# Moving a block's routing counts one step later in a mixture-of-experts kernel

## The chip, the cores and the metric

The kernel runs on one core of a Trainium2 chip. The metric is device time in microseconds, from the start of the program to its end. Before the change three runs took 1308.88, 1309.06 and 1309.46 us; the median is 1309.06 us. A core has a matrix engine (TensorE, "PE" in the profile, with its weight loads as "PEld"), three engines for elementwise work (VectorE "DVE", ScalarE "ACT", GpSimd "POOL"), and SyncE ("SP"), which in this kernel issues nearly all plain DMA transfers. Each engine works through its own instructions in a fixed order.

## What is computed

For 8192 tokens of width 512, the layer normalizes the input `x`, adds a random-feature attention of the normalized tokens, and adds a mixture of 64 experts, of which every token uses 8 (with 256 places per expert), plus a shared expert. Cut to what matters here:

```python
xn = _layernorm(x)
# attention: features of every token times features of a weight
feats = 1/sqrt(512) * AB * exp(xn @ (ab*proj).T - 0.5*|xn|^2 * ab^2)
attn  = feats @ weights.T
# routing
scores      = sigmoid(xn @ router_w)              # 64 experts in 8 groups
masked      = scores of the 4 best groups, 0 elsewhere
topk_w, topk_idx = top_k(masked, 8);  topk_w = 2.5 * topk_w / sum(topk_w)
onehot = one_hot(topk_idx.reshape(-1), 64)
prior  = cumsum(onehot, axis=0) - onehot          # how many came before, per expert
pos    = prior at the chosen expert               # the token's place in the expert's list
# each expert works on its list; results are weighted and added back
out = x + attn + experts(xn) + shared_expert(xn)
```

The running count of tokens per expert (`prior`) is what the changed step builds, block by block.

## The kernel before

The 8192 tokens are cut into 16 blocks of 512 (`NB`, `TB`), a block into four pieces of 128. All matrix products are done in three parts (upper times upper, upper times rest, rest times upper), which `products` (L103) issues; `upper` (L97) makes the upper part on ScalarE and `rest` (L100) the remainder on VectorE.

**Two phases.** In the first, to about 400 us, `dense` (L517) does the shared expert and the attention for the even blocks 0, 2, ..., 14, and beside it every block, odd ones too, is normalized, turned and routed. In the second, the 64 experts run one after another (`hidden` L796, `down` L817), with the attention of the odd blocks and the last block's dense part put between them.

**Steps.** `dense` is a generator. For one even block it yields ten times: n = 0 and 1 after the two halves of the shared expert's hidden layer (24 products each, `ps_gu`), n = 2 to 5 after four feature chunks (12 products each, `ps_f`), n = 6 to 9 after four output pieces (18 products each, `ps_o`). After every yield the main loop (L867) calls `routing(step)` (L853), with steps counted 0 to 79; so two blocks are routed for each even block of dense work, one every five steps (`GAP`).

**What `routing` does in a step.** It first advances every running `look_up` generator by one yield, in order of blocks. Then, on the block's first step (second for block 1), it starts `look_up` for the next block. In its third step of five it computes the statistics and normalizes one block ahead (`normalize`, L299, into the `xw` tiles), and in the second it loads a block two ahead (`load_tokens`).

**Stages of `look_up(b)` (L345), one per step:**

- turn: 16 transposes into `ps_x`, split into `xT_h` (ScalarE) and `xT_l` (VectorE, L101); odd blocks store both to `turned`
- logits: 8 products into `ps_l`, copied to `lt`; the squared norms are stored by four small DMAs (`as_row`, L258)
- back: four transposes into `ps_lt`, sums `lg`, exponentials into the `xw` tiles
- groups: the penalty that rules out all but the 4 best groups
- top 8: `top`, `mask_r`, and the running sums `prior_r` (L437) and `taken` (L440), all on VectorE
- a step in which nothing is done
- **counts**: five products into `ps_bu` (L447, L458), of which the first gives counts before the block and the others the counts within it; the second kind is copied to `cu` (ScalarE, L466) and stored to `upto` (L467); then the shares of the chosen experts (L469 to L475), and the two stores of the normalized rows and their shares to `xnw` (L478)
- `begun` (L486): two VectorE updates from the first count

Counted from a block's turn as step 0, the counts come at step 6. For odd blocks from 3 on the turn follows the dense step n = 0, so that the counts come at n = 6; for even blocks the turn follows n = 5 and the counts come at n = 1 of the next dense block.

**What sets the order.** The program order gives each instruction a rank. The framework that builds the program then plays it through with estimated durations and gives each engine the ready instruction of the best rank; the result is a fixed order per engine. An instruction whose data are ready early can thus go before others that stand before it in the program. `behind(a, b)` (L119) forces a to come after b: `counted` comes after the last product of the dense step (L454), and so do the transposes of `ps_lt`.

**Buffers that matter.** `ps_sm` has two PSUM buffers, shared by `ps_x` (every second one), `ps_l`, `ps_lt`, `ps_bu` and, later, `ps_fu` and `ps_y`. `mask` and `prior` have one buffer each, `top` two. The `xw` tiles have four buffers of which each block takes two, from its normalization to the landing of its `xnw` stores.

**The hand-over.** In the last dense block, after n = 8, `chunks` (L691) turns `begun` into row numbers, and `find` and `gather` (L699, L752) start to look up each expert's tokens with indirect DMAs. They need the last block's counts.

Of the kernel before, what the change touches and what calls it, by code (L numbers as in the profile page):

```python
# [32 lines left out]
NB = T // TB  # L33
# [20 lines left out]
def rfs_attention_moe_kernel(  # L54
# [290 lines left out]
    def look_up(b):  # L345
# [94 lines left out]
        nc.vector.tensor_tensor(taken, prior[:, NS - 1, :], mask[:, NS - 1, :], ALU.add)  # L440
        yield
        yield


        both = ps_sm.tile([P, 2, TB // 2], FP, tag="sm", name="ps_bu")
# [210 lines left out]
    for rc in range(RC):  # L656
        pool, tag = ((ps_sm, "sm"), (ps_tr, "tr"))[rc // 2]
        ps_w.append(pool.tile([P, H], FP, tag=tag, name="ps_f"))
        projected(parts(wT, KC), rc, ps_w[rc])
    late = look_up(0)  # L660
    next(late)
    upper0 = last["upper"]
# [190 lines left out]
    def routing(t):  # L853

        for b in sorted(fronts):
            if next(fronts[b], fronts) is fronts:
                del fronts[b]
        b, k = divmod(t + GAP, GAP)
        if k == (b == 1) and b < NB:
            fronts[b] = look_up(b)  # L860
            next(fronts[b])
        if k == GAP - 3 and b + 1 < NB:
            normed[b + 1] = normalize(b + 1, *roots(b + 1, statistics(xbs[b + 1])))
        if k == 1 and b + 2 < NB:
            xbs[b + 2] = load_tokens(b + 2)
# [140 lines left out]
```

## Time and profile before

| What | Value |
|---|---|
| Median of three runs | 1309.06 us |
| Profiled execution | 1309.75 us |
| its span | 1308.0 us |
| DVE busy in the span | 71% |
| DMA, mean over the span | 259 GB/s |
| First and last count product (L447), start | 48.9 and 392.8 us |

The profile is of one execution. Its views used here are: the page (busy time by engine, granted TensorE clock in 40 slices), the timeline (start, duration, engine, line, operation, what is written and read, and in brackets the idle time just before and what ended it), the waits (who waited for whom), the chain of waits (followed back from the last instruction), and the times at which DMA transfers landed. In the timeline equal neighbours are merged ("x4" is four instructions). The end of a matrix product is modelled, so its start is the sounder number: 512-column products that follow each other without a gap start 0.227 us apart.

### The profile page before, as it was taken

To read this page: it belongs to the slowest core of one execution; us is meant where nothing else is said; L and a number is where in the kernel's file an instruction comes from. 1 tells how busy PE (TensorE), PEld (TensorE's weight loads), DVE (VectorE), ACT (ScalarE), POOL (GpSimd) and SP (SyncE) were. 2 spreads that over 40 slices of the span, in tenths; PEclk is the share of its full clock that TensorE was granted. 3 is DMA by queue.
4 is the path that set the end of the run, shared out by engine and by line. 5 is a ranking of instruction groups with operands and counts; after the bars stand their busy time and mean duration, and the time that the engine had idled before them with its cause. 6 is when DMAs were issued, how large, how long until landed. Compare 5 with 4: busy or idle time off the path is not lost.

```text
span 1308.0 us, 21401 instructions
## 1 busy us (share of the span) xinstructions
PE 1295.1 (99%) x7648; PEld 1136.1 (87%) x7648; DVE 925.9 (71%) x1922; ACT 644.1 (49%) x1017; POOL 587.0 (45%) x692
## 2 busy tenths in 40 slices
PE   8999999999999999999999999999999999999998
PEld 6888888888888988999999999999999999988886
DVE  7978768867765776678677677777776776643555
ACT  5643544454432555566566465656665565540111
POOL 3122022123106766777677767767766654210000
PEclk9999999999999999999999999999999999999999
DMA  7655675675586989999999999999999999784995
GB/s 255 242 209 207 242 282 200 240 286 212 198 306 191 308 236 322 263 288 274 303 288 251 282 290 270 264 302 290 275 257 297 286 260 238 204 240 167 319 319 193
DMA packets 189498, 338.61 MB, mean 259 GB/s; under 512 B 15952, under 2 KB 87632, under 8 KB 189392
## 3 DMA queue, kind: packets, MB, share of 16 engines
q1 hardware_dynamic: 153456, 245.93, 54.4%
q0 software_dynamic: 35936, 91.32, 29.8%
q8 instruction: 60, 0.98, 0.3%
q14 instruction: 46, 0.38, 0.1%
HBM read 220.66 MB, written 104.99 MB: 249 GB/s over the span
## 4 chain that ended last, share of the span: by engine, by line
PE 87%; DVE 7%; DMA 3%; SPq 1%; issue 1%; ACT 1%; POOL 0%; ACTq 0%; DVEq 0%
PE ps_gu L108 41%; PE ps_e L108 13%; PE ps_o L108 12%; PE ps_fu L108 6%; PE ps_y L108 5%; PE ps_t L773 3%; PE ps_f L108 3%; PE ps_x L333 2%; PE ps_l L366 1%; DMA xb<-in_L_attn_x_dram 1%; DVE st L277 1%; DVE f L495 1%; SPq L264 1%; DVE xT_l L101 1%; DVE fT L101 1%
## 5 line engine op out<-in xcount | busy, mean ns | idle before, releaser
L831 POOL DMA_INDIRECT out_dram<-ye,who x128 | 232.7, 1818 | 181.5 <-ACT ye L830 120.8
L108 PE MATMUL ps_gu<-gT,gu_h 128*128 128x256 f32 x2048 | 292.5, 285 | 0.0
L108 PEld LDWEIGHTS ps_gu<-gT,gu_h 128*128 128x128 f32 x2048 | 265.4, 190 | 8.9 <-ACT gu_h L98 4.7
L703 POOL DMA_INDIRECT at<-upto,line x128 | 131.9, 1030 | 76.0 <-DVE first_of L697 37.3
L101 DVE TENSOR_TENSOR gu_l<-gu,gu_h 128x1024 fp32r<-128x1024 f32 x128 | 155.0, 1221 | 14.3 <-ACT gu_h L98 13.4
L108 PE MATMUL ps_gu<-gT,gu_l 128*128 128x256 f32 x1024 | 164.9, 283 | 0.0
L756 POOL DMA_INDIRECT xg<-xnw,who x128 | 141.7, 1107 | 40.0 <-issue 30.0
L108 PE MATMUL ps_e<-d_h,ehT 128*128 128x512 f32 x512 | 147.8, 390 | 0.0
L108 PEld LDWEIGHTS ps_gu<-gT,gu_l 128*128 128x128 f32 x1024 | 142.6, 191 | 3.4 <-DVE gu_l L101 0.7
L98 ACT CAST gu_h<-gu 128x1024 fp32r<-128x1024 f32 x128 | 132.1, 1047 | 0.0
L830 ACT ACTIVATE ye<-ps_e,we 128x512 f32<-128x512 f32 x128 | 87.6, 687 | 84.5 <-PE ps_e L108 84.2
L108 PEld LDWEIGHTS ps_e<-d_h,ehT 128*128 128x128 f32 x512 | 94.7, 188 | 18.8 <-ACT d_h L98 0.2
L98 ACT CAST ehT<-sg 128x512 fp32r<-128x512 f32 x64 | 39.9, 623 | 123.1 <-DVE sg L503 112.0
L248 POOL TENSOR_TENSOR a<-rstd,ve 128x4 f32<-128x4 f32 x45 | 10.2, 227 | 200.5 <-DVE rstd L244 198.0
L503 DVE SCALAR_TENSOR_TENSOR sg<-sg,ps_gu 128x512 f32<-128x512 f32 x64 | 43.9, 686 | 72.1 <-PE ps_gu L108 72.0
L101 DVE TENSOR_TENSOR gT<-ps_t,gT 128x512 fp32r<-128x512 f32 x128 | 82.0, 682 | 17.1 <-ACT gT L98 17.1
L101 DVE TENSOR_TENSOR d_l<-d,d_h 128x1024 fp32r<-128x1024 f32 x64 | 78.2, 1221 | 11.7 <-ACT d_h L98 11.6
L509 ACT ACTIVATE f<-f,ab 128x512 f32<-128x512 f32 x64 | 46.3, 723 | 73.1 <-DVE f L495 72.4
L108 PE MATMUL ps_o<-fW_h,fT 128*128 128x512 f32 x288 | 79.8, 391 | 0.2 <-ACT fT L98 0.2
L108 PE MATMUL ps_e<-d_l,ehT 128*128 128x512 f32 x256 | 79.2, 390 | 0.0
L108 PE MATMUL ps_o<-d_h,hT 128*128 128x512 f32 x256 | 79.1, 396 | 0.0
L501 ACT ACTIVATE sg<-ps_gu 128x512 f32<-128x512 f32 x64 | 38.2, 597 | 77.7 <-PE ps_gu L108 77.7
(181 smaller groups left out, 2520.0 us busy)
## 6 DMA issues: line engine op xcount, KB each, us to landing
gu<-in_L_ffn_gate_w_dram SPq DMA_DIRECT2D x64, 512.0 KB
gu<-in_L_ffn_up_w_dram SPq DMA_DIRECT2D x64, 512.0 KB
d<-in_L_ffn_down_w_dram SPq DMA_DIRECT2D x64, 512.0 KB
xnw<-xw SPq DMA_DIRECT2D x32, 577.0 KB
xb<-in_L_attn_x_dram SPq DMA_DIRECT2D x32, 512.0 KB
out_dram<-xb SPq DMA_DIRECT2D x32, 512.0 KB
xT_h<-turned SPq DMA_DIRECT2D x30, 512.0 KB
xT_l<-turned SPq DMA_DIRECT2D x30, 512.0 KB
```

What stands on the lines that cost most here:

```text
L98: return nc.scalar.copy(dst, src)
L101: return on.tensor_tensor(dst, src, hi.bitcast(FP), ALU.subtract)
L108: last["pe"] = nc.tensor.matmul(ps, w[c][a], v[c][b], start=(start and part == 0 and c == 0), stop=(stop and part == 2 and c == n - 1),)
L333: last["turn"] = nc.tensor.transpose(pr[:, ts(s, P)], src(s)[:, ts(kc, P)], ident if dt is FP else ident_r)
L501: nc.scalar.activation(dst, g, AF.Tanh, scale=0.5)
L503: nc.vector.scalar_tensor_tensor(dst, dst, 0.5, u, ALU.mult, ALU.mult)
L509: nc.scalar.activation(f, f, AF.Exp, scale=ab[:, rc : rc + 1])
L703: nc.gpsimd.indirect_dma_start(out=at[:, e % TE, h, :], out_offset=None, in_=upto, in_offset=bass.IndirectOffsetOnAxis(ap=line[:, e, h : h ...
L756: nc.gpsimd.indirect_dma_start(out=xgs[e][:, h, :], out_offset=None, in_=xnw, in_offset=bass.IndirectOffsetOnAxis(ap=who[:, e, h : h + 1], ...
L773: turned_s = nc.tensor.transpose(pr[:, c, ts(h, P)], xr[:, h, ts(c2 * 2 + c, P)], ident_r)
L830: nc.scalar.activation(ye[:, h, :], po, AF.Copy, scale=wes[e][:, h : h + 1])
L831: now = nc.gpsimd.indirect_dma_start(out=out, out_offset=bass.IndirectOffsetOnAxis(ap=who[:, e, h : h + 1], axis=0), in_=ye[:, h, :], in_o ...
```

## The change

A third bare `yield` is put before the counts for all blocks but the last one:

```diff
         nc.vector.tensor_tensor(taken, prior[:, NS - 1, :], mask[:, NS - 1, :], ALU.add)
         yield
         yield
+        if b < NB - 1:
+
+            yield
 
 
         both = ps_sm.tile([P, 2, TB // 2], FP, tag="sm", name="ps_bu")
```

Whatever follows in `look_up` (the count products, `cu`, `upto`, the shares, the `xnw` stores, and `begun` in the step after) comes at step 7 and 8 rather than 6 and 7, counted from the turn. For odd blocks the counts then follow the dense step n = 7, and for even blocks n = 2. Block 15 keeps steps 6 and 7. No instruction is added or removed.

## The prediction

> **What bounds the kernel now.** I read the page first, then the granted clock by slice, then the start times of the matrix products in the timeline, then who waited for whom around the counts, and last the chain of waits.
>
> ```profile
> span 1308.0 us, 21401 instructions
> PE 1295.1 (99%) x7648; PEld 1136.1 (87%) x7648; DVE 925.9 (71%) x1922; ACT 644.1 (49%) x1017; POOL 587.0 (45%) x692
> PEclk9999999999999999999999999999999999999999
> ```
>
> TensorE is busy for 99% of the span at full clock (mean 0.999). Since the ends of products are modelled, I checked this by starts: products of 512 columns start 0.227 us apart (the median of the trace). Summing what any start is later than that, the routing phase after the opening (60 to 430 us) has hardly a gap over 0.1 us. Those that repeat stand in one place, before the first count of every second block:
>
> ```profile
> 204.63 0.61 PE L108 MATMUL ps_o<-fW_h,fT 128*128 128x512 f32 x2
> 205.43 0.36 PE L447 MATMUL ps_bu<-prior_r,ones_r 128*128 128x256 f32 x1 [0.19 <-DVE prior_r L437]
> ...
> 206.02 0.45 PE L366 MATMUL ps_l<-xT_h,rwp 128*128 128x512 f32 x1
> ```
>
> The second of two products starts at 204.86, so the count could start at 205.09 and starts at 205.43: 0.34 us lost. What it waits for is the last sum of prior counts on VectorE:
>
> ```profile
> 205.07 0.21 DVE L437 TENSOR_TENSOR prior_r<-prior_r,mask_r 128x64 fp32r<-128x64 f32 x1
> 205.21 0.68 DVE L550 TENSOR_TENSOR xb<-ps_o,xb 128x512 f32<-128x512 f32 x1
> ```
>
> It ends at 205.29, 0.14 us before the count. In the same way blocks 5, 7, 9, 11 and 13 lose 0.19, 0.34, 0.36, 0.45 and 0.49 us (counts at 158.28, 205.43, 252.62, 299.96, 347.32): **1.84 us**. The even blocks lose nothing: there the sums end 7 to 12 us before their count (171.76 against 183.98).
>
> **What moves.** For blocks 0 to 14, everything between the bare yields and the end of `look_up` comes a step later: five products, the copy `cu`, its store `upto`, the exponential of `top`, five VectorE instructions for the shares, two `xnw` stores, and two updates of `begun` in the step after. Nothing is added or removed. A step is 24, 12 or 18 products of 0.227 us: 5.4, 2.7 or 4.1 us.
>
> *Counts of odd blocks.* They go from behind the first `ps_o` step to behind the second, 4 us on. The sums are then 4 us old; the wait goes. What is late next? `ps_l` of the next block moves up to 205.09. Its first four products read `xT_h` (last ScalarE copy done at 202.1); the four with `xT_l` come 0.9 us later, at 206.0, and the last `xT_l` ends at 205.15. So nothing takes the wait's place: −1.84 us.
>
> Here a rule speaks against me. The Trainium skill, "Perfetto Trace Analysis", section Optimization Strategy, says that the same gap repeating on an engine that should be saturated can mean that there is no SBUF or PSUM buffer for the next tile. The count takes one of two `ps_sm` buffers, and after the change count and `ps_lt` share them. By the rule moving it would gain 0. The row names `prior_r`; the two VectorE reads that free the banks end at 204.42 and 205.15, before the sum's 205.29, and `ps_lt` needs only the bank that `ps_l` leaves when its copy is made, which it needs anyway. I take 1.84.
>
> *Counts of even blocks.* From behind the second `ps_gu` step to behind the first `ps_f`. The 0.5 us of products only trade places. `cu` (0.36 us) and the two `begun` (0.87 us) fall at about 189 to 191 us. ScalarE idles there until 190.12, and VectorE has this gap:
>
> ```profile
> 191.53 0.69 DVE L101 TENSOR_TENSOR fT<-f,fT 128x512 fp32r<-128x512 f32 x1 [1.45 <-ACT fT L98]
> ```
>
> 1.45 us idle against 0.87 us: free. Without this cover it is up to 1.2 us per block.
>
> *SyncE's queue.* The even block's count store moves past four `norms` stores and two loads of `xb`:
>
> ```profile
> 185.82 0.37 SPq L467 DMA_DIRECT2D upto<-cu  x1
> 186.28 2.66 SPq L264 DMA_DIRECT2D norms<-sq  x4
> 188.99 0.91 SPq L151 DMA_DIRECT2D xb<-in_L_attn_x_dram  x2
> 192.78 1.74 SPq L163 DMA_DIRECT2D out_dram<-xb  x2
> ```
>
> The store holds back `norms` until `cu` is made; this falls away, so the loads can only come earlier, as far as their buffers allow. Value 0, as TensorE has no gap left. GpSimd's queue: nothing that moves is issued there.
>
> *Share columns and `xnw` stores.* The `xw` tiles have four buffers, two per block, so `normalize` of block b+2 waits for the stores of block b. Does their issue move? In before, even blocks' stores are issued at 171.9 and 173.1 us though the program has them with the counts at 184: instructions go when their data are there, not by step. I expect them to stay. For odd blocks the share arithmetic (205.94 to 207.7) finds only lower-priority statistics as competitors afterwards; it stays within about 0.5 us. Bounds: 0, and 4.1 us if they do wait for the step. Even then: stores at 160.5 us land at 165.6 and would land at 169.7; `normalize` starts at 167.35 and its second tile at 169.17; the copies `xc` land at 174.3 and TensorE turns that block at 177.1. A delay of up to 2.4 us is hidden by 2.8. Cost 0.
>
> *Block 0 and 1.* Here VectorE is full (5.00 of 5 us in each window from 35 to 70) and buffers are short:
>
> ```profile
> 57.22 0.88 SPq L478 DMA_DIRECT2D xnw<-xw  x2
> ...
> 63.41 1.52 ACT L303 ACTIVATE xw<-xb,shift,rstd 128x512 f32<-128x512 f32 x2 [1.34 <-DMA xnw<-xw]
> ```
>
> Block 2's normalization waits for block 0's second store, and TensorE lost 0.30 us on it at 64.28. One step later lets the next feature's subtraction (0.68 us, now at 57.17) go ahead of the shares: 0.7 us, all on the path. Ends: 0 (order by readiness) and 2.7 (a whole `ps_f` step). The rule and the row differ: "DMA: Bandwidth & Descriptors", section Anatomy of one DMA (fitted on GpSimd's path), gives 2.0 us plus bytes over 436 GB/s, for 577 KB an estimate of 3.4 us. Then the store issued at 57.68 would be in at 61.0, before the first tile is normalized at 62.1, and the delay costs nothing. The chain of waits has 5.70 us for this store. The row decides: **+0.7 us**. Block 1's stores (72.2 us, landing 79.4; block 3 is turned at 82.52 with 0.5 us to spare) have nothing new ahead on VectorE: 0, at worst 4.1 − 0.5 = 3.6.
>
> *The single `mask` and `prior` buffers.* The next block's first write of `prior_r` (L435, 206 us and later) waits 4 us more; its sums come 12 us later. 0.
>
> *Hand-over.* Block 15 is exempt, so `begun`, `line` and the first searches keep their place. Block 14's updates of `begun` (0.87 us) go into 378 to 381 us, where VectorE idled 2.31 and 1.50 us: 0; at worst 0.87 on the chain of features that ends in TensorE's 0.37 us gap at 389.89.
>
> **Sum.** −1.84 + 0.7 = −1.1 us. The profiled execution took 1309.75 us (span 1308.0 and 1.75 around it), giving 1308.6. It lies 0.69 above the median of the runs, so against that: 1309.06 − 1.1 = **1307.9 us**.
>
> **Rivals.**
> *A, slower: the count store gets ahead of the loads.* Place: SyncE, every even block. New count at 183.98 + 1.9 (`ps_l`) + 2.7 (`ps_f`) = 188.6, products 0.5, `cu` until 189.7, the store done at 190.1: loads 1.1 us after 188.99. They feed the statistics that VectorE does at 192.79, and the run of VectorE work behind them ends in `fT` and `xT_l`. The fourth `fT` is copied at 201.11, TensorE uses it at 201.46: 0.35 us of slack, and beyond that it decides. (1.1 − 0.35) × 6 pairs = 4.5, so 1309.06 + 4.5 − 1.1 = 1312.4; with `norms` behind it too, 3.8 us late, some 20 us more. Against: program order has the loads first. For: the store now becomes ready just as they do.
> *B, slower: the stores of blocks 0 and 1 do wait a step.* 2.7 + 3.6 − 1.84: 1313.5. For: full VectorE, buffers short. Against: even blocks' early stores.
> *C, slower: the covers fail.* `cu` and `begun` land in VectorE's full stretch: (1.23 − 0.35) × 6 = 5.3, less 1.1: 1313.3.
> *D, faster:* the earlier loads also close the gaps at 46.08, 64.28, 70.90, 389.89 and 426.35 (0.26, 0.30, 0.21, 0.37, 0.28): 1.84 + 1.42 = 3.3: 1305.8. For: these waits lie downstream of VectorE. Against: three lie before any load has moved.
> *E, it does little:* a wait for `xT_l` or a bank replaces the one removed: 1309.1.
>
> **Numbers.** Forecast 0.40, E 0.08, D 0.12, A 0.15, B 0.13, C 0.12. Within 0.2% (2.6 us, what a measurement can tell here) are forecast and E: 0.48; faster is D: 0.12; slower A, B and C: 0.40. The forecast's own range, with its unknowns, is 1306.9 to 1310.0. Both signs hold much, so the range reaches to 1306.2 below (cutting D's end) and 1316 above (A with `norms` late left out).
>
> **What would show it.** Right: counts of odd blocks start within 0.02 us of the product before them plus 0.227; `ps_l` without a gap; `xnw` stores at their old distance from the products; loads of `xb` no later than 5.0 us after the second `ps_gu` step. A: the store of counts between `norms` and loads, gaps before `ps_o`. B: ScalarE waiting longer than 1.34 us for `xnw` near 63 us, a gap before block 2's or 3's turn. C: `begun` between 193 and 206 us. I am wrong altogether if the search phase, 430 us on, gets gaps from a changed order of buffers, which I can't see from here.

## The result, and the profile after

| | before | after |
|---|---|---|
| Median of five runs | 1309.46 us (1308.88 to 1310.26) | 1321.79 us (1320.58 to 1324.15) |
| Profiled execution, its span | 1309.75, 1308.0 us | 1321.45, 1319.7 us |
| Block 15's first count product, start | 392.76 us | 404.13 us |

The five runs of before are the three named above and two more. The ratio is **1.0097**, 95% interval 1.0086 to 1.0108: 12.3 us slower. Block 15's first count product, the last of the routing phase, starts 11.4 us later, so nearly all of the loss lies ahead of it. First the page of after (busy time by engine, granted clock by slice, shares of the chain that ended last):

```profile
span 1319.7 us, 21417 instructions
PE 1297.9 (98%) x7648; PEld 1138.5 (86%) x7648; DVE 928.2 (70%) x1922; ACT 645.5 (49%) x1017; POOL 583.3 (44%) x692
PEclk9999999999999999999999999999999999999999
...
PE 81%; DVE 7%; DMA 5%; POOL 3%; issue 2%; ACT 1%; SPq 1%; POOLq 0%; ACTq 0%; DVEq 0%
```

Busy times have hardly moved; the span grew by 11.7 us and TensorE's busy time by 2.8. (The 16 instructions more than before are semaphore waits; every engine does as many operations as before.) The chain is more telling: TensorE had 87% of it before, and now DMA (3% before) and GpSimd (below 1%) take part. Which transfer it is, the waits of after between 60 and 420 us say (who waited for whom; total us, times, longest):

```profile
POOL xc L316 <- ACT xw L303: 64.4, 11, 11.3
...
PEld ps_x L333 <- DMA xc<-xw: 10.3, 7, 2.5
...
PE ps_x L333 <- DMA xc<-xw: 9.0, 6, 2.4
```

No wait of TensorE for `xc` stands in the answer of before, and `ps_bu`'s wait for `prior_r`, 1.0 us there, is gone. `xc` is the copy of a block's normalized rows that the turn reads; two DMAs of 512 KB in GpSimd's queue make it (L316). Here is the turn of block 7 in the timeline of TensorE, in before:

```profile
177.11 1.49 PE L333 MATMUL ps_x<-ident_r,xc 128*128 128x128 f32 x16
178.44 1.16 PE L108 MATMUL ps_gu<-xT_h,gu_h 128*128 128x512 f32 x4
```

and in after:

```profile
181.04 1.07 PE L108 MATMUL ps_gu<-xT_h,gu_l 128*128 128x512 f32 x4
181.94 0.28 PE L333 MATMUL ps_x<-ident_r,xc 128*128 128x128 f32 x2
184.59 1.40 PE L333 MATMUL ps_x<-ident_r,xc 128*128 128x128 f32 x14 [2.36 <-DMA xc<-xw]
185.82 1.55 PE L108 MATMUL ps_gu<-xT_h,gu_h 128*128 128x512 f32 x4
187.17 1.91 PE L108 MATMUL ps_gu<-xT_l,gu_h 128*128 128x512 f32 x4
188.88 1.51 PE L108 MATMUL ps_gu<-xT_h,gu_l 128*128 128x512 f32 x4
190.22 1.09 PE L108 MATMUL ps_gu<-xT_h,gu_h 128*128 128x512 f32 x4
```

Two losses are in the rows of after. The third transpose starts 2.65 us after the first where two transposes need some 0.17: a gap of 2.49 by starts. And three lots of four products start 1.35, 1.71 and 1.34 us apart in place of 0.91, together 1.7 us. A table of stretches shows why (columns: stretch, its length, busy time of five engines, granted TensorE clock, share of the DMA engines, GB/s):

```profile
core 0: us, PE busy (x) PEld busy (x) DVE busy (x) ACT busy (x) POOL busy (x), PEclk, DMA share, GB/s
178.00:182.00 4.00, 4.00 (x20) 3.21 (x19) 0.69 (x1) 0.60 (x1) 0.00 (x0) 1.00 1.02 375
182.00:185.00 3.00, 0.64 (x8) 0.50 (x6) 1.38 (x2) 0.63 (x2) 0.00 (x0) 1.00 0.98 370
185.00:186.50 1.50, 1.50 (x15) 1.42 (x14) 0.89 (x2) 1.50 (x4) 0.00 (x0) 0.96 0.04 12
186.50:190.00 3.50, 3.50 (x11) 2.68 (x10) 1.72 (x4) 1.95 (x4) 0.72 (x1) 0.53 0.90 357
190.00:193.00 3.00, 3.00 (x15) 2.46 (x14) 0.69 (x1) 2.01 (x3) 0.27 (x1) 1.00 1.00 391
```

The granted clock is 0.53 for 3.5 us after the gap. The page's 40 slices are 33 us wide and show 9 throughout, and the mean clock is 0.996: such a dip is seen only in a fine window.

The turns of blocks 5, 7, 9, 11 and 13 have such gaps: 2.96 (in two parts), 2.49, 1.15, 1.16 and 2.07 us by starts, **9.8 us**. Slower products follow only after blocks 5 and 7, some **3.3 us** for both. Less the 1.84 us of gaps before `ps_bu` that are gone, and with some 0.5 us elsewhere: 9.8 + 3.3 − 1.8 + 0.5 = 11.8, against the span's 11.7.

**Why the copies come late.** GpSimd's timeline around block 7's copies in before (whole rows, those of the same small operations left out):

```profile
167.56 0.22 POOL L296 TENSOR_SCALAR padded<-q 128x4 f32<-128x4 f32 x1
169.17 0.78 POOL L316 DMA_DIRECT2D xc<-xw  x1 [1.38 <-ACT xw L393]
169.97 0.21 POOL L248 TENSOR_TENSOR a<-rstd,ve 128x4 f32<-128x4 f32 x1
...
171.05 0.77 POOL L316 DMA_DIRECT2D xc<-xw  x1 [0.31 <-ACT top L469]
171.84 0.25 POOL L251 TENSOR_TENSOR rstd<-a,rstd 128x4 f32<-128x4 f32 x1
```

and in after:

```profile
170.62 0.47 POOL L296 TENSOR_SCALAR padded<-q 128x4 f32<-128x4 f32 x1
171.07 0.34 POOL L248 TENSOR_TENSOR a<-rstd,ve 128x4 f32<-128x4 f32 x1
...
175.81 0.22 POOL L296 TENSOR_SCALAR padded<-q 128x4 f32<-128x4 f32 x1
176.38 1.50 POOL L316 DMA_DIRECT2D xc<-xw  x2 [0.34 <-issue]
```

GpSimd computes 1/sqrt of a block's variances by small operations (L248 to L251 three times, then `shift`, `q` and `padded`): a *root*, 17 operations some 0.28 us apart, 5 us in all. In before the copies of block 7 stand between block 7's root and block 8's, with three operations of the latter between them. In after all of block 8's root stands ahead of both copies, though `xw` is ready at 173.7 us. Then a second delay comes on top: SyncE issues three transfers of its own, two of them stores of block 6's `xnw`, between 176.72 and 179.3, and the copies meet these. (In the table, "turn" is the start of the first transpose.)

| Copies of block 7 | before | after |
|---|---|---|
| issued | 169.17, 171.05 | 176.38, 177.15 |
| landed, after | 3.15, 3.21 us | 5.43, 7.39 us |
| landed at | 172.32, 174.27 | 181.80, 184.54 |
| turn | 177.11 | 181.94 |

Over all 22 copies the median from issue to landing is 4.7 us before and 6.1 after.

### The profile page after: what moved, and what is told of

Its sections match the earlier page's. It is cut to its first block, busy times and chain, and to the rows that moved or that the text cites. A ratio compares the mean times of both kernels' runs of the same rounds, so it can differ in the third digit from the quotient of the medians.

```text
span 1319.7 us, 21417 instructions
## 1 busy us (share of the span) xinstructions
PE 1297.9 (98%) x7648; PEld 1138.5 (86%) x7648; DVE 928.2 (70%) x1922; ACT 645.5 (49%) x1017; POOL 583.3 (44%) x692
## 4 chain that ended last, share of the span: by engine, by line
PE 81%; DVE 7%; DMA 5%; POOL 3%; issue 2%; ACT 1%; SPq 1%; POOLq 0%; ACTq 0%; DVEq 0%
PE ps_gu L108 38%; PE ps_e L108 13%; PE ps_o L108 10%; PE ps_y L108 5%; PE ps_fu L108 5%; PE ps_f L108 4%; PE ps_t L776 3%; DMA xc<-xw 3%; PE ps_x L333 1%; PE ps_l L366 1%; DVE st L277 1%; POOL at L706 1%; DMA xnw<-xw 1%; DVE f L498 1%; DVE fT L101 1%
## 5 line engine op out<-in xcount | busy, mean ns | idle before, releaser
L834 POOL DMA_INDIRECT out_dram<-ye,who x128 | 226.1, 1767 | 185.4 <-ACT ye L833 116.3
L248 POOL TENSOR_TENSOR a<-rstd,ve 128x4 f32<-128x4 f32 x45 | 10.6, 235 | 191.5 <-DVE rstd L244 173.1
L101 DVE TENSOR_TENSOR gT<-ps_t,gT 128x512 fp32r<-128x512 f32 x128 | 82.1, 683 | 17.1 <-ACT gT L98 17.1
L101 DVE TENSOR_TENSOR d_l<-d,d_h 128x1024 fp32r<-128x1024 f32 x64 | 78.2, 1222 | 11.7 <-ACT d_h L98 11.6
```

The source lines that it names most:

```text
L101: return on.tensor_tensor(dst, src, hi.bitcast(FP), ALU.subtract)
L834: now = nc.gpsimd.indirect_dma_start(out=out, out_offset=bass.IndirectOffsetOnAxis(ap=who[:, e, h : h + 1], axis=0), in_=ye[:, h, :], in_o ...
```

## The experiments

Theory **Q**: the loss comes from the copies' place in GpSimd's queue; put back, it is gone. **C**, a part of it: the copies, once late, also collide with the `xnw` stores. Rivals: **B**, later share columns and stores hold up the `xw` buffers; **A**, the counts' store in SyncE's queue holds up the loads; **L**, it is the queue place alone, without a collision. The theories of each run are named anew in its expectation.

Runs e1 to e10 were made on three other chips, on which the kernel before took 1332 to 1333 us, so each is compared by its ratio to the kernel before on the same chip. Their traces have gaps behind 405 us, at the hand-over, which those of before and after on the first chip don't have. The start of block 15's first count product ("count 15": 392.76 before, 404.13 after) shows the routing phase without them. No trace of the kernel before was taken on these three chips; e7, which has no gap at a turn, has 391.64. "Gaps" are summed by starts.

| Run | Ratio (95%) | count 15 | gaps at odd turns | gaps before `ps_bu` |
|---|---|---|---|---|
| after, first chip | 1.0097 (1.0086 to 1.0108) | 404.13 | 9.8 | 0 |
| e11, after again | 1.0119 (1.0104 to 1.0135) | 403.85 | 9.6 | 0 |
| e12, before again | 1.0000 (0.9991 to 1.0008) | 392.56 | 0 | 1.8 |
| e1, after, tied | 0.9981 (0.9971 to 0.9992) | 390.69 | 0 | 0 |
| e7, before, tied | 1.0000 (0.9981 to 1.0020) | 391.64 | 0 | 1.6 |
| e2, counts alone late | 1.0130 (1.0107 to 1.0152) | 411.51 | 14.6 | 0 |
| e3, shares and stores alone late | 1.0000 (0.9985 to 1.0015) | 394.34 | 0.3 | 2.6 |
| e4, odd blocks alone | 1.0022 (1.0009 to 1.0035) | 393.79 | 1.8 | 0 |
| e10, even blocks alone | 1.0018 (1.0007 to 1.0029) | 392.65 | 0 | 2.0 |
| e8, odd blocks alone, tied | 0.9982 (0.9969 to 0.9994) | 391.60 | 0 | 0 |
| e6, before, 15 operations ahead of copies | 1.0195 (1.0169 to 1.0221) | 419.50 | 18.4 | 0 |
| e9, before, 8 operations ahead of copies | 0.9998 (0.9980 to 1.0017) | 393.68 | 0.9 | 1.3 |
| e5, after, stores kept apart | 1.0036 (1.0022 to 1.0049) | 397.81 | 0.5 | 0 |

**e1: the copies put back in their place.** After, with the first operation of a root on GpSimd forced behind the last copy issued:

```diff
-            on.tensor_tensor(a, y, v, ALU.mult)
+            begin = on.tensor_tensor(a, y, v, ALU.mult)
+            if on is nc.gpsimd and "xc" in last:
+                behind(begin, last.pop("xc"))
...
-                nc.gpsimd.dma_start(t, w[:, :, :H])
+                last["xc"] = nc.gpsimd.dma_start(t, w[:, :, :H])
```

> The changed kernel, with one order added on GpSimd: the reciprocal root of the next block may not start before the two xc copies of the block before it are issued. Theory Q (the xc copies of odd blocks stand behind a whole root in GpSimd's queue, 5 us, and land too late for the turn): the gaps before ps_x and the half clock go, the gain at the counts stays, 1307 to 1309 us. Theory B (xw buffers come free a step later, normalize is late): no change, 1320 to 1323 us.

Measured: 0.9981, faster than before. GpSimd's timeline of e1 has block 7's copies ahead of block 8's root again:

```profile
167.91 0.78 POOL L318 DMA_DIRECT2D xc<-xw  x1 [1.53 <-PE ps_o L108]
169.33 0.72 POOL L318 DMA_DIRECT2D xc<-xw  x1 [0.64 <-ACT xw L305]
170.07 0.21 POOL L248 TENSOR_TENSOR a<-rstd,ve 128x4 f32<-128x4 f32 x1
```

and block 7's turn is without a gap, in TensorE's timeline of e1:

```profile
176.32 1.07 PE L108 MATMUL ps_gu<-xT_h,gu_l 128*128 128x512 f32 x4
177.23 1.47 PE L335 MATMUL ps_x<-ident_r,xc 128*128 128x128 f32 x16
178.54 1.16 PE L108 MATMUL ps_gu<-xT_h,gu_h 128*128 128x512 f32 x4
```

Everything that the change moves in the program is still moved here, the stores too. Q holds; A and B fall as causes of the loss.

**e7: the same tie on the kernel before.** The diff is that of e1, on the kernel before. Is the tie itself worth something?

> The kernel before, with the order on GpSimd that e1_tied has (roots behind the copies). If the order added on GpSimd brings e1_tied's gain by itself: ratio 0.998. If the gain comes from the counts: ratio 0.999 to 1.001, and the gaps at ps_bu stay.

Measured: 1.0000, and the gaps before `ps_bu` stay (1.6 us). The tie alone brings nothing; what e1 has over before is the moved counts. The view of the count products by tile (here of e1; duration min/median/max in ns, then the idle time before them, of which there is none to list; in before the same view lists 1.0 us for `prior_r`) shows that their wait went:

```profile
L452 PE MATMUL ps_bu<-prior_r,ones_r x16: 280/280/282, 52.2 to 390.7; 128*128 128x256 f32 x16
its engine sat idle before it (us, times) until:
who waited for it (us, times):
  ACT cu L471: 29.2, 8
```

**e2 and e3: the change in two halves.** In e2 the shares and the `xnw` stores keep their step and the counts come a step later; in e3 the counts keep theirs.

```diff
 e2
+        nc.scalar.activation(top, top, AF.Exp, scale=-1.0)
...
+        if b < NB - 1:
+            yield
         both = ps_sm.tile([P, 2, TB // 2], FP, tag="sm", name="ps_bu")
 e3
         nc.sync.dma_start(upto[ts(b, NS * E), :].rearrange("(q p) t -> p q t", p=P), cu)
-
+        if b < NB - 1:
+            yield
         nc.scalar.activation(top, top, AF.Exp, scale=-1.0)
```

> Of the moved work only the count products, cu, upto and begun come a step later; the shares and the xnw stores keep their step. Theory B (late xnw stores hold the xw buffers): 1307 to 1309 us. Theory Q, if moving the counts alone turns GpSimd's order over, as its built order has it (roots ahead of four xc copies from block 7 on): 1316 to 1322 us, gaps before ps_x as in the changed kernel.

> Only the shares and the xnw stores come a step later; the counts and begun keep their step. Theory B: 1316 to 1322 us. Theory Q: the built order keeps the xc copies of odd blocks between parts of the root, the second one behind two thirds of it, so at most small gaps before ps_x: 1309 to 1312 us, with the gaps at ps_bu still there.

Measured: e2 1.0130, e3 1.0000. All of the loss comes with the counts, which touch neither `xw` nor `xc`. In e2 block 7's copies are issued at 171.28 and 172.05 us, right behind the whole root of block 8, land 5.98 and 8.07 us later, and TensorE waits for both, as its timeline of e2 shows:

```profile
177.30 0.36 PE L333 MATMUL ps_x<-ident_r,xc 128*128 128x128 f32 x2 [1.17 <-DMA xc<-xw]
180.17 1.40 PE L333 MATMUL ps_x<-ident_r,xc 128*128 128x128 f32 x14 [2.51 <-DMA xc<-xw]
```

More is lost than in after, since the copies are issued 4.7 and 3.9 us ahead of the time at which the turn was due (175.97, the product before it plus 0.227), against 5.6 and 4.8 in after; the expectation was too low here.

**e4 and e10: odd blocks alone, even blocks alone.**

```diff
 e4
+        if b % 2 and b < NB - 1:
+
+            yield
 e10
+        if b % 2 == 0:
+
+            yield
```

> Only odd blocks get the third bare yield. Theory Q: in the built order their xc copies come before the last third of the root, so they are late by 3 us rather than 5; gaps at ps_bu gone (1.8 us), gaps before ps_x small: 1307 to 1311 us. Theory B: the odd blocks' xw buffers are the ones that bind, so as slow as the changed kernel, 1320 us.

> Only even blocks' counts come a step later. In the built order the first xc copy of an odd block stands behind two thirds of a root, the second one behind all of it. Theory Q: the gaps at ps_bu stay, small gaps of up to 1 us before the turn of odd blocks: ratio 1.001 to 1.005. If the even blocks' counts are what costs in the changed kernel by SyncE's queue (rival A of the prediction): ratio 1.007 to 1.010 with gaps before ps_o.

Measured: 1.0022 and 1.0018; neither makes much of the loss alone. In e4 the gaps before `ps_bu` go as predicted. The copies of blocks 7 to 13 stand behind six of the 17 operations of the next root (block 7's issued at 170.54) and are in time; only block 5's turn is late, by 1.8 us, and its second copy stands behind a whole root. In e10 the copies stand behind eight and eleven operations and no turn waits. The count of operations goes with the loss in all the runs that only move work: all five late turns of after, the four of e2 (block 5's copies have none ahead there, and its turn is in time) and the one of e4 have all 17 ahead of the second copy, and with eleven or fewer no turn lost more than 0.3 us. So the loss is not a sum of parts but a threshold that the two shifts cross together. e4's 0.2% is more than its count 15 (1.0 us later) accounts for, and e10's count 15 is no later at all, so the rest of these two ratios lies behind the routing phase and was not looked into.

**e8: odd blocks alone, tied.** e4 with e1's tie.

> Only odd blocks' counts a step later, and the order on GpSimd added. The gaps at ps_bu are all at odd blocks, and block 0 keeps its step: ratio 0.997 to 0.999, as good as e1_tied or 0.5 us better. If ps_l of the next block now waits for xT_l as in e4_odd (gaps of 0.3 us): 0.999.

Measured: 0.9982, as e1. The move of the even blocks brings nothing that these intervals (some 0.1% to either side) can tell; the odd blocks' 1.84 us are enough for the whole gain. Two gaps of 0.4 us before `ps_l`, which waits for `xT_l`, show that in this arrangement a little of it is taken back.

**e6 and e9: nothing but a late copy.** In the kernel before, 15 or 8 small GpSimd operations that compute nothing of use are put ahead of each odd block's copies:

```diff
+            if b % 2:
+                spin = rt.tile([P, NS], FP, tag="spin", name="spin", bufs=1)
+                nc.gpsimd.tensor_copy(spin, shift)
+                for _ in range(14):
+                    spun = nc.gpsimd.tensor_scalar(spin, spin, 1.0, None, ALU.mult)
             for t, w in zip(xc, xw):
-                nc.gpsimd.dma_start(t, w[:, :, :H])
+                copied = nc.gpsimd.dma_start(t, w[:, :, :H])
+                if b % 2:
+                    behind(copied, spun)
```

with `range(7)` in e9.

> The kernel before, its counts where they were; GpSimd does 15 small operations (some 4.2 us) ahead of the xc copies of each odd block, and nothing else is changed. Theory Q with C: copies issued near 171.8 us rather than 169.2, together with the even block's xnw stores at 171.9 and 173.1, landing 5 to 8 us later; gaps of 1 to 3 us before the turn of odd blocks; ratio 1.005 to 1.011. Rival (it was some other part of the changed order, and GpSimd's delay is harmless): ratio 0.999 to 1.001.

> As e6_delay with half the delay: 8 small operations (some 2.2 us) ahead of the xc copies of odd blocks, which would be issued near 170 us and 172 us. If lateness costs only beyond a slack (the prediction's 2.8 us before the turn) and the second copy just meets the even block's stores: gaps of at most 1 us before ps_x, ratio 1.000 to 1.004. If each us of delay costs alike: half of e6_delay's loss, ratio 1.009 to 1.010.

Measured: e6 1.0195, e9 0.9998. So lateness of the copies is enough by itself, without any moved count. (The added operations hold up the next root too; TensorE has no new gaps from that, only those at the turns.) In e6 block 7's copies are issued at 176.50 and 178.39 us, 4.5 and 2.6 ahead of the time at which the turn was due (181.01), and TensorE's timeline of e6 has after's gap:

```profile
181.62 0.36 PE L340 MATMUL ps_x<-ident_r,xc 128*128 128x128 f32 x2 [0.45 <-DMA xc<-xw]
184.51 2.02 PE L340 MATMUL ps_x<-ident_r,xc 128*128 128x128 f32 x14 [2.52 <-DMA xc<-xw]
```

Half of the delay costs 0.9 us at one turn and nothing else (block 7's copies are issued at 170.52 and 172.41 and land 3.2 and 5.3 us later, the second at 177.7, with the turn at 177.60); the whole delay costs 18 us of gaps. The slack ends about where e9 stands. e6 came out dearer than expected, since all six of its odd turns from block 5 on are late and the granted clock fell to half after each.

**e5: the collision alone taken away.** After, in which the `xnw` stores of even blocks wait until the copies issued before them have landed:

```diff
+            last["copies"] = [
+                nc.gpsimd.dma_start(t, w[:, :, :H]) for t, w in zip(xc, xw)
+            ]
...
+            if b % 2 == 0:
+                for c in last.get("copies", ()):
+                    tc.add_manual_dep(stored.ins, c.ins.name, AFTER, reason="apart")
```

> The changed kernel, GpSimd's order left as it is (a whole root ahead of the xc copies of odd blocks); only the xnw stores of even blocks wait until the xc copies of the odd block have landed, so that the two don't share the DMA engines. Theory C (late issue and collision together: without it a copy lands 3.2 to 3.9 us after its issue, 1 us before the turn needs it): ratio to before 0.998 to 1.001, no gap before ps_x. Theory L (the late issue alone is enough): gaps before ps_x stay, ratio 1.007 to 1.010.

Measured: the gaps at the turns shrink from 9.8 to 0.5 us. Block 7's copies, still behind the whole root and issued just as far ahead of the turn as in after (173.48 and 174.25, the turn at 179.04: 5.6 and 4.8), land 3.95 and 4.47 us later, in time. So C holds and L falls: the queue place alone would have been borne; queue place and collision together are not. But the wait has a price of its own, 1.0036: it stands in SyncE's queue, and the loads of `xb` behind it come late: the first lands 17.1 us after block 7's turn, where before has 15.7 and e1 14.8, and VectorE's statistics wait 1.88 us for it, until 196.16. SyncE's waits and TensorE's in e5 (second fence):

```profile
SPq L482 <- DMA xc<-xw: 63.8, 12, 11.0
```

```profile
PEld ps_o L108 <- ACT fT L98: 6.8, 7, 1.7
...
PE ps_o L108 <- ACT fT L98: 3.9, 6, 1.3
```

New gaps before `ps_o` and `ps_l` take the place of those before `ps_x`. That the late loads make these gaps is argued from the order of the rows. The expectation had not counted this.

**e11 and e12: after and before once more**, without an edit, to see what a ratio is worth and whether the other chips' gaps matter.

> The changed kernel as it is, on a chip on which the kernel before takes some 1332 us and not 1309. Q (the late copies cost what they cost in the routing phase, whatever the chip does later): ratio 1.008 to 1.011, block 15's first count product at about 404 us, gaps before the turns 9 to 11 us. H (the gaps at the hand-over, which this chip has and the first has not, take up part of the loss or add to it): ratio below 1.006 or above 1.013.

> The kernel before against itself: what a ratio is worth here. Ratio 1.000 with an interval of about 0.001 to each side; an interval that leaves out 1 would say that the differences of 0.2% in other runs aren't to be trusted. Block 15's first count product at 392.8 us as on the first chip if the routing phase is the same there; the 23 us that this chip takes longer then lie behind 400 us.

Measured: this time the kernel before took 1309.65 us, so H stays open. e12's ratio is 1.0000 with some 0.0008 to either side: on that chip differences of 0.2% can be told. On the three others the intervals are 0.1 to 0.2% to either side, so that e1's gain is clear of noise, but its size is known only roughly. e11 is 1.0119, somewhat above the first measurement's interval, with the same picture: count 15 at 403.85, clock 0.52 and 0.50 after the turns of blocks 5 and 7. The change costs 1.0 to 1.2%.

## Why the prediction was wrong, point by point

The forecast was 1307.9 us, and measured were 1321.79, above the range too.

- **Odd blocks' counts, −1.84 us: right.** The gaps went in every version that moves these counts (after, e1, e2, e4, e8), and stayed where it doesn't (e3, e10). With the copies in place e1 is 2.5 us faster than before (1 − 0.9981 of 1332.94; 1.1 to 3.9 by the interval). The rule on repeating gaps, weighed there, would have given 0; the row that named `prior_r` was the better guide.
- **Even blocks' counts, 0: right in time.** e8, without them, is as fast as e1. `begun` runs at 190.67 us in e1, in the place named.
- **SyncE's queue, 0: right.** In after `norms` goes at 189.11, the loads of `xb` at 192.99 and the counts' store only at 199.55. Rival A does not occur.
- **"GpSimd's queue: nothing that moves is issued there": this is the step that failed.** The sentence is true and the conclusion is not. No instruction on GpSimd changed its step, but the order there is made by readiness, and what feeds GpSimd did change: VectorE sends it the seed of each root (L244). With block 5's `begun` (0.94 us) out of their way the statistics are done sooner, and block 8's seed goes ahead of block 6's group work on VectorE (from L391 on) instead of amid it. VectorE in before and after (second fence):

```profile
164.33 0.42 DVE L391 TENSOR_TENSOR lt<-ps_lt,lt 128x256 f32<-128x256 f32 x1
166.38 0.16 DVE L244 TENSOR_SCALAR rstd<-rstd 128x4 int32<-128x4 int32 x1
```

```profile
168.83 0.17 DVE L244 TENSOR_SCALAR rstd<-rstd 128x4 int32<-128x4 int32 x1
169.69 0.41 DVE L391 TENSOR_TENSOR lt<-ps_lt,lt 128x256 f32<-128x256 f32 x1
```

Counted from block 6's turn, block 8's seed comes at 15.6 us in before and at 13.0 in after, so the next root is ready sooner and goes ahead of block 7's copies: they are issued 5.6 and 4.8 us ahead of the turn and not 7.9 and 6.1, meet the stores, and five turns lose 9.8 us in gaps and some 3.3 in slow products. That the order turned and what it cost is shown (e1, e6); that the earlier seed turned it is argued. For it: the seed comes at 15.1 us in e4 (six operations ahead of the second copy), at 13.9 in e10 (eleven) and at 13.1 in e2 (all 17). Against: in e3 it comes at 15.7, as in before, and six are ahead, not three. The order is fixed beforehand from estimated durations, which no trace shows, so this step stays open.

- **The `xnw` stores keep their place: right.** Block 5's stores are issued 9.85 us after block 6's turn (165.64 and 155.79 us), before 9.73 (160.50 and 150.77). e3, where only these are put a step later, costs nothing.
- **"A delay of up to 2.4 us is hidden by 2.8": the slack was right, and applied to the wrong thing.** Landing 174.3 and turn 177.1 were the right rows, and e9, in which the second copy of block 7 lands just at the turn, uses it up without loss. But it was held only against late stores, not against the copies' own queue. In after the copies of block 7 are issued 5.6 and 4.8 us ahead of the turn, before 7.9 and 6.1. The second thus loses 1.3 us of lead, and its landing takes 4.2 us more: 5.5, less the slack of 2.8, is the gap within 0.2 us. The lead alone, 1.3 us, would have been borne.
- **Block 0 +0.7, block 1 0: right within the noise.** Block 0's stores went 1.4 us later, and from block 1's turn to block 2's logits it took 0.3 us more than before in one pair of profiles and 0.6 in the other (e11 against e12). ScalarE's wait of 1.34 us became two, of 0.87 and 1.09. Block 1's stores went 2.4 us later and no gap followed.
- **Single buffers and hand-over, 0: right within 0.3 us.** One gap at 401.26 us, where before had 0.37, is 0.66 long.

None of the rivals had the mechanism. D's gain did not come, and A, B and C were slower for reasons that the runs exclude. The order of SyncE's and GpSimd's queues in the new program couldn't be read off the change, but the slack of each transfer that feeds a turn could, and the copies' 2.8 us was already on the page of working.

## What to carry to other kernels

Where a framework orders each engine by readiness, moving work on one engine can turn the order on an engine on which nothing moved: list every in-order queue that feeds the next stage, DMA issues behind small operations above all, and the slack of each. Count that slack against queue place and collision together, since each alone may be borne. When a step is moved, pin the orders that the old timing happened to give: one forced order here turned a loss of 1.0% into a gain of 0.2% (each against the kernel before on its own chip; the gain's interval is 0.1 to 0.3%).

## What the runs showed of the hardware

**The clock after short gaps.** In after the granted clock was 0.50 from 135.17 to 138.59 us and from 186.37 to 189.79, and 1.00 on both sides of these. In all traces each stay at half clock up to 400 us lasts 3.41 us or twice that, and two in one trace start a multiple of 3.41 us apart (in after 51.20, 15 times 3.41). In after, e2, e4, e9 and e11 the clock stayed at 1.00 after a turn where the idle time in its brackets added up to 1.94 us or less (eight turns), and fell to half where it was 2.36 us or more (eight turns). e6 has one exception, where it fell after 1.81 us. Where a gap lies against the steps of 3.41 us may count too (all of e6's 1.81 us lies between two of them, and of after's 1.94 us at 331.06 at most 1.3), but what exactly is reckoned stays open. The Trainium skill, "TensorE: Matmul & The Clock Gate", section What's actually happening, has the clock halved after an idle window of about 3.4 us. The half clock agrees; so much idle time was not needed: 2.36 us in all were enough here. By the page no gap of after (2.96 us at most) would have cost more than itself, and 3.3 us would be missing from the sum.

**Transfers that meet.** In before block 7's copies of 512 KB land 3.2 us after their issue, with the DMA engines at a share of 0.45 while the first is under way. In after the two copies, two stores of 577 KB and one of 512 KB are under way at once: 2.75 MB, an estimate of 7.3 us at the 375 GB/s of the table above, in which the share is 0.98 to 1.02. The last copy took 7.39 us, and in e2, in the same crowd, 8.07: the copy that comes last waits for nearly the whole crowd. In e2 the packets of block 7's first copy, issued at 171.28, begin to move only at 174.64; until then one store of 577 KB and one of 512 KB from SyncE's queue have the DMA engines to themselves. The Trainium skill, "DMA: Bandwidth & Descriptors", section Queues, rings and completion order, says that each DMA engine takes turns between the rows it has work for, which fits copies issued from one queue being slowed by stores from another.

**Chips.** The kernel before took 1309 to 1310 us in the first measurement and beside e11 and e12, and 1332 to 1333 on three other chips. The traces from these have gaps at the hand-over, such as 6.58 us at 420.99 and 6.33 us at 441.26 in e1. The cause was not looked for.
